# Layer 1 of a four-layer kernel: how the planes a and b go to HBM and come back

## The chip, the cores and the metric

One core of one Trainium2 chip runs the whole program in one launch. The metric is the device time of an execution in microseconds (us). The core has a matrix engine (TensorE, PE; its weight loads are listed as PEld), three engines for elementwise work (VectorE, DVE; ScalarE, ACT; GpSimd, POOL), SyncE (SP), which here only issues DMAs, and 16 DMA engines, which move data between HBM and the on-chip memory (SBUF, 128 partitions). Matmul results land in PSUM.

## The reference, cut to what matters

The input x has 256 x 256 tokens of 128 channels. Four layers follow each other, each `x = x + layer(groupnorm(x))`: triangle attention (layer 0), a triangle multiplication over 16 channels (layer 1), a second one over 128 channels (layer 2), and a chain of convolutions (layer 3). The change lies in layer 1:

```python
a = jax.nn.sigmoid((x @ Wa1 + ba1) * (x @ Wa2 + ba2))   # 16 channels
b = jax.nn.sigmoid((x @ Wb1 + bb1) * (x @ Wb2 + bb2))
g = jax.nn.sigmoid(x @ Wg + bg)
z = jnp.einsum('bikc,bkjc->bijc', a, b)                 # per channel: a 256 x 256 times 256 x 256 product
return g * (_ln(z, ln2_g, ln2_b) @ Wz + bz)
```

All data are float32. The products with the weights need x with channels on the partitions; the product in `z` needs, for each of the 16 channels, a whole 256 x 256 plane with tokens on the partitions. Between the two, a and b go through HBM.

## The kernel before, in words

The 65,536 tokens are cut into 32 pieces of 2048 (`SC`), a piece into four chunks of 512 (`CK`). The layers run one behind the other. In layer 1 the engines' orders are written out by hand (`manual_schedule`): instructions run on each engine in the order of the code. The whole stage is three loops.

*Making a and b (pool `p3`, lines 828 to 877).* The result of layer 0, channels by tokens, lies in HBM as `x1T`. Thirteen slots in SBUF hold pieces of it; eight are loaded before the loop (line 778, `load1`), five at its head, and the loop over pieces, with index i, loads piece i+13 into the slot that piece i has left. For a piece, eight groups of matmuls (line 859) with 32 output rows each (16 of a, 16 of b) write the four chunks q of both factors to partitions 32q to 32q+31 of two PSUM tiles `p1`, `p2`. ACT copies the first with its bias (line 868), DVE multiplies by the second (line 869), and one step later ACT takes the sigmoid into `p3_ab` (line 842, `close3`), a tile of 128 x 512 of which there are 12 buffers. Row 32q + c holds channel c (0 to 15 of a, 16 to 31 of b) of chunk q. `store3` (line 848) sends it to HBM three steps after the piece's matmuls: four DMAs of 32 rows, those for q = 0 and 1 on POOL's queue, those for q = 2 and 3 on SP's. Each row is 2 KB. So on SP a step issues the load of piece i+13, then two stores for piece i-3. After the last load, which is followed by the stores of piece 15, only stores are left.

The tensor `abD` in HBM has 32 rows, one per channel, each 65,536 tokens long plus 1024 of padding; within a row the order is chunk number q, then piece s, then the 512 tokens t of the chunk.

*The product (pool `z`, lines 881 to 936).* Channels are taken in pairs g. `load_z(g)` fetches two planes of a and two of b into one of three buffers: both planes of a by one DMA of 512 KB (line 893; a row's 128 stretches of 512 tokens go to the 128 partitions in the order in which they lie, so partition 32q + s holds chunk q of piece s), and each plane of b by one of 256 KB in the order of the tokens (line 895; partition 4s + q). Three pairs are fetched ahead; a later one, k // 2 + 3, after the second plane k of a pair. For each plane, four transposes on PE turn a (`tri_turn`, line 1807), ACT copies the result (line 1809), and eight matmuls multiply (`tri_multiply`, line 1818). The transposes of plane k+1 stand ahead of the product of plane k. DVE, ACT and POOL collect sums for the layer norm (lines 914 to 926); the sixteen planes are normalized and sent to HBM (line 936).

*The last loop (pool `p4`)* multiplies by `Wz`, applies the gate and adds to x.

Two rules set the order of the DMAs. The first load of a waits for all stores to `abD`. And the build gives each queue's DMAs eight semaphores in turn, so a DMA on SP is issued only when the one eight places before it on SP has landed; POOL's DMAs have eight of their own. A sigmoid waits until the store of the piece twelve before it has landed, because it writes the same buffer.

The parts of the code that the change touches:

Of the kernel before, what the change touches and what calls it, by code (L numbers as in the profile page):

```python
# [9 lines left out]
F32 = mybir.dt.float32  # L10
# [6 lines left out]
P = 128  # L17
N = 256
D = 128
T = N * N  # L20
SC = 2048
NSC = T // SC
CK = 512
NH = 4
HC = 32
PAD = 1024
# [6 lines left out]
def kernel(ctx: ExitStack, tc: tile.TileContext, a: dict, out: bass.AP):  # L33
    nc = tc.nc
# [4 lines left out]
    dram = ctx.enter_context(tc.tile_pool(name="dram", bufs=1, space=DRAM))  # L39

    def rows(name, n):

        return dram.tile([n, T + PAD], F32, name=name)[:, 0:T]
# [3 lines left out]
    rsD = dram.tile([1, T], F32, name="rsD")  # L47
    mbD = dram.tile([N, N], F32, name="mbD")
    x1T = rows("x1T", D)
    abD = rows("abD", 32)  # L50
    znD = rows("znD", 16)
    x2T = rows("x2T", D)

# [184 lines left out]
    with tc.tile_pool(name="x0", bufs=1) as xres, tc.tile_pool(name="p0", bufs=3) as sb:  # L238
        held = {s: xres.tile([P, SC], F32, name=f"x0_{s}") for s in range(RES, NSC)}
        with tc.tile_pool(name="p0ps", bufs=3, space=PSUM) as ps, tc.tile_pool(  # L240
            name="f0ps", bufs=2, space=PSUM
# [167 lines left out]
        with tc.tile_pool(name="p1", bufs=2) as wk_sb, tc.tile_pool(  # L409
            name="p1ps", bufs=4, space=PSUM  # L410
# [70 lines left out]
    with tc.tile_pool(name="p2e", bufs=6) as eb, tc.tile_pool(name="p2c", bufs=1) as cs:  # L481
        triT = cs.tile([P, NH, 2, N], F32, name="triT")
        with tc.tile_pool(name="p2", bufs=2) as sb, tc.tile_pool(
            name="p2S", bufs=2, space=PSUM
        ) as psS, tc.tile_pool(name="p2z", bufs=1, space=PSUM) as psZ, tc.tile_pool(
            name="p2M", bufs=3, space=PSUM
        ) as psM, ExitStack() as by_hand:
            groups = {}
            rows = {}
# [213 lines left out]
            for j in range(2 * NG + 5):  # L703
                g, half = divmod(j, 2)
# [71 lines left out]
    def load1(s, slot):  # L776
        xs[s] = slots[slot].tile([P, SC], F32, name="x1", tag="x1")
        nc.sync.dma_start(xs[s], x1T[:, s * SC : (s + 1) * SC])
# [54 lines left out]
    with x1_scope:  # L833
        with tc.tile_pool(name="p3", bufs=3) as sb, tc.tile_pool(
            name="p3ps", bufs=3, space=PSUM
        ) as ps, tc.manual_schedule():
            halves, done = [], []

            def close3():
                s, s1 = halves.pop(0)  # L840
                ab = sb.tile([P, CK], F32, name="p3_ab", bufs=12)
                nc.scalar.activation(ab, s1, AF.Sigmoid)
                done.append((s, ab))

            def store3():
                s, ab = done.pop(0)
                for q in range(4):
                    (nc.gpsimd if q < 2 else nc.sync).dma_start(
                        abD.rearrange("c (q s t) -> q s c t", q=4, t=CK)[q, s], ab[32 * q : 32 * q + 32, :]
                    )  # L850

            for i in range(FIRST, SLOTS):
                load1(order1[i], i)
            for i, s in enumerate(order1):
                p1 = ps.tile([P, CK], F32, name="p3_1")
                p2 = ps.tile([P, CK], F32, name="p3_2")
                for pp, w in ((p1, v1), (p2, v2)):
                    for c in range(4):
                        nc.tensor.matmul(
                            pp[32 * c : 32 * c + 32, :], lhsT=w, rhs=xs[s][:, c * CK : (c + 1) * CK],  # L860
                            start=True, stop=True,
                        )
                if i + SLOTS < NSC:
                    load1(order1[i + SLOTS], i % SLOTS)
                if len(done) > 1:
                    store3()
                s1 = sb.tile([P, CK], F32, name="p3_s1")
                nc.scalar.activation(s1, p1, AF.Identity, bias=vb1)
                nc.vector.scalar_tensor_tensor(s1, p2, vb2, s1, ALU.add, ALU.mult)
                halves.append((s, s1))  # L870
                if i:
                    close3()
            close3()
            while done:
                store3()
# [4 lines left out]
        with tc.tile_pool(name="z", bufs=2) as sb, tc.tile_pool(  # L880
            name="zps", bufs=3, space=PSUM
        ) as ps, tc.manual_schedule():
            Z = sb.tile([P, 16, 2 * N], F32, name="z_Z", bufs=1)
            s1 = sb.tile([P, 2 * N], F32, name="z_s1", bufs=1)
            s2 = sb.tile([P, 2 * N], F32, name="z_s2", bufs=1)
            base = sb.tile([P, 2 * N], F32, name="z_base", bufs=1)
            AB = {}

            def load_z(g):
                if g < 8:  # L890
                    ab = gate_pool.tile([P, 4, 2 * N], F32, name="z_ab", tag="g")
                    AB[g] = A, B = ab[:, 0:2, :], ab[:, 2:4, :]
                    nc.sync.dma_start(A, abD[2 * g : 2 * g + 2, :].rearrange("c (p t) -> p c t", p=P))
                    for c in range(2):
                        nc.sync.dma_start(
                            B[:, c, :], abD[16 + 2 * g + c, :].rearrange("(q s t) -> s q t", q=4, t=CK)
                        )

            def turn_z(k):
                if k < 16:  # L900
                    return tri_turn(nc, ps, sb, AB[k // 2][0], k % 2, ident, nc.scalar.copy)

            for g in range(3):
                load_z(g)
            nc.vector.memset(Z[:, 0, :], 0.0)
            at = turn_z(0)
            for k in range(16):
                nxt = turn_z(k + 1)
                pz = tri_multiply(nc, ps, at, AB[k // 2][1], k % 2).rearrange("p t n -> p (t n)")
                at = nxt  # L910
                if k % 2 == 1:
                    load_z(k // 2 + 3)
                if k == 0:
                    nc.vector.tensor_copy(base, pz)
                    continue
                z = Z[:, k, :]
                nc.vector.tensor_tensor(z, pz, base, ALU.subtract)
                sq = s2 if k == 1 else sb.tile([P, 2 * N], F32, name="z_sq")
                nc.scalar.activation(sq, z, AF.Square)
                if k == 1:  # L920
                    nc.vector.tensor_copy(s1, z)
                    continue
                nc.vector.tensor_tensor(s1, s1, z, ALU.add)
                if k < 15:
                    nc.gpsimd.tensor_tensor(s2, s2, sq, ALU.add)

            nc.vector.scalar_tensor_tensor(s1, s1, -1.0 / 16, s1, ALU.mult, ALU.mult)
            nc.vector.tensor_tensor(s2, s2, s1, ALU.add)
            nc.vector.tensor_tensor(s2, s2, sq, ALU.add)
            nc.vector.tensor_scalar(s2, s2, 0.0, None, ALU.max)  # L930
            nc.scalar.activation(s2, s2, AF.Sqrt, bias=epst, scale=1.0 / 16)
            nc.vector.reciprocal(s1, s2)
            for q in range(4):
                zq = Z[:, 4 * q : 4 * q + 4, :]
                nc.vector.tensor_tensor(zq, zq, s1.unsqueeze(1).to_broadcast([P, 4, 2 * N]), ALU.mult)
                nc.sync.dma_start(znD[4 * q : 4 * q + 4, :].rearrange("c (p t) -> p c t", p=P), zq)
# [4 lines left out]
        with tc.tile_pool(name="p4", bufs=3) as sb, tc.tile_pool(  # L941
            name="p4psg", bufs=2, space=PSUM
# [46 lines left out]
            for i, s in enumerate(order):  # L989
# [5 lines left out]
                for c in range(4):  # L995
                    q = slice(32 * c, 32 * c + 32)
# [83 lines left out]
    with tc.tile_pool(name="x5", bufs=7) as x5_pool, tc.tile_pool(name="p5", bufs=2) as sb, tc.tile_pool(name="p5psX", bufs=1, space=PSUM) as psX, tc.tile_pool(  # L1080
        name="p5psM", bufs=3, space=PSUM
# [89 lines left out]
        for s in range(NSC):  # L1171
            b, j = divmod(s, KB)
            load5(s + 7)
            ab = [sb.tile([P, SC], F32, name=n) for n in ("p5_a", "p5_b")]
# [55 lines left out]
    with tc.tile_pool(name="p6", bufs=3) as sb, tc.tile_pool(name="p6ps", bufs=3, space=PSUM) as ps:  # L1230
        nc.vector.memset(k1, 0.0)
        nc.gpsimd.memset(k2, 0.0)
        with tc.manual_schedule():
# [16 lines left out]
            for c in range(D):  # L1250
                q = c // 4
# [21 lines left out]
    with tc.tile_pool(name="p7", bufs=2) as sb, tc.tile_pool(name="p7psX", bufs=2, space=PSUM) as psX, tc.tile_pool(  # L1273
        name="p7psM", bufs=2, space=PSUM
# [142 lines left out]
    with tc.tile_pool(name="p9", bufs=2) as sb, tc.tile_pool(name="p9psM", bufs=2, space=PSUM) as psM, tc.tile_pool(  # L1417
        name="p9psX", bufs=2, space=PSUM
# [382 lines left out]
def tri_turn(nc, ps, sb, A, c, ident, evacuate):  # L1801

    Ac = A[:, c, :].rearrange("p (t k u) -> p t u k", t=2, u=2)
    pa = ps.tile([P, 2, N], F32, name="tp_a")
    for u in range(2):
        for t in range(2):
            nc.tensor.transpose(pa[:, u, t * P : (t + 1) * P], Ac[:, t, u, :], ident)  # L1807
    at = sb.tile([P, 2, N], F32, name="tp_at")
    evacuate(at, pa)  # L1809
    return at  # L1810


def tri_multiply(nc, ps, at, B, c):
    Bc = B[:, c, :].rearrange("p (u n) -> p u n", u=2)
    pz = ps.tile([P, 2, N], F32, name="tp_z")
    for t in range(2):
        for u in range(2):
            nc.tensor.matmul(  # L1818
                pz[:, t, :], lhsT=at[:, u, t * P : (t + 1) * P], rhs=Bc[:, u, :], start=(u == 0), stop=(u == 1)
            )  # L1820
    return pz
# [38 lines left out]
```

## Time and profile before

Four runs took 3407.88 to 3417.56 us, with a median of 3410.55.

| | |
|---|---|
| profiled execution | 3411.61 us |
| its span (first to last instruction) | 3409.9 us |
| mean granted PE clock | 0.957 |
| busy share of the span: PE, DVE, ACT, POOL | 92%, 66%, 59%, 47% |
| loop that makes a and b | from about 1505 to 1589 us |
| loop of the product | from about 1589 to 1628 us |
| stores to `abD` | 64 from POOL, 64 from SP, 64 KB each |
| issue of one such store on POOL | 496 ns |
| loads from `abD` | 8 of 512 KB (a), 16 of 256 KB (b) |

Times are from the start of the span. In the rows of a timeline, the first two numbers are start and length in us, then come engine, line, operation, output <- input, how many equal ones were merged (x), and in brackets how long the engine had been idle and what ended that. "SPq" is the queue of SP: the length there is that of issuing DMAs, not that of the transfers. In the window table each row is a stretch of time, with the busy time and the number of instructions of each engine, the granted clock of PE (1.00 is full), the mean busy share of the 16 DMA engines, and the rate at which they moved data. The busy share of a whole execution is a mean over stages with different limits; the two loops here take about 120 of the 3410 us.

### The profile page before, as it was taken

Reading aid. Unit: us, or ns where it says so; the run is one execution under the profiler, and the core shown is the slowest. Engines: PE = TensorE matmul, PEld = TensorE weight load, DVE = VectorE, ACT = ScalarE, POOL = GpSimd, SP = SyncE. Lnnn points to the kernel's source line nnn. Section 1 sums busy time; section 2 is a strip of 40 time slices with the busy share of each in tenths; the row PEclk is TensorE's granted clock in tenths of the full one; section 3 lists DMA queues with packets and bytes.
Section 4 is the critical chain, followed back from the end, with each engine's and each line's share of the span. In section 5 each row is a group of like instructions: output and inputs, shape, how many; then the busy total and the mean of one; then the engine's idle time right before and its main releaser. Section 6 shows DMA issues by size and latency. Waiting matters only on the chain. (4 is left out here: it accounts for less than half of the span.)

```text
span 3409.9 us, 52669 instructions
## 1 busy us (share of the span) xinstructions
PE 3121.2 (92%) x20266; PEld 1649.6 (48%) x20266; DVE 2263.1 (66%) x2608; ACT 2014.1 (59%) x2204; POOL 1618.6 (47%) x930
## 2 busy tenths in 40 slices
PE   5669999999999999966886999999999999769998
PEld 5425555555555555523332444444999433224444
DVE  5627888888888888843554545444555677747776
ACT  3657777777777777733575444443444466636565
POOL 4146777777777777733463000000555344514334
PEclk8889999999999999978996999999999999979999
DMA  9972333333333333278596668756999899756664
GB/s 393 365 292 72 122 110 119 107 119 109 117 114 112 119 107 119 95 302 317 213 380 269 260 224 298 284 210 252 349 353 350 304 336 334 277 165 198 202 197 131
DMA packets 298235, 750.06 MB, mean 220 GB/s; under 512 B 74954, under 2 KB 145580, under 8 KB 248828
## 3 DMA queue, kind: packets, MB, share of 16 engines
q1 hardware_dynamic: 289371, 734.19, 60.3%
q0 software_dynamic: 8096, 10.86, 0.9%
q8 instruction: 162, 2.65, 0.3%
q10 hardware_dynamic: 512, 1.59, 0.1%
q14 instruction: 94, 0.76, 0.1%
HBM read 458.88 MB, written 287.66 MB: 219 GB/s over the span
## 5 line engine op out<-in xcount | busy, mean ns | idle before, releaser
L564 DVE TENSOR_TENSOR p_e<-p_S,triT 128x1024 f32<-128x1024 f32 x512 | 608.9, 1211 | 144.9 <-PE p_S L554 144.9
L574 POOL TENSOR_TENSOR p_es<-p_e 128x1024 f32<-128x1024 f32 x256 | 603.5, 2369 | 126.2 <-issue 66.6
L572 ACT ACTIVATE p_e<-p_e,mbT 128x1024 f32<-128x1024 f32 x512 | 552.0, 1138 | 61.3 <-DVE p_e L564 61.2
L1152 PE MATMUL p_pm<-p_zn,wf 128*128 128x512 f32 x1040 | 450.2, 595 | 1.4 <-DVE p_zn L1169 1.4
L539 PE MATMUL p_mm<-p_xn,w 128*128 128x512 f32 x768 | 407.3, 614 | 0.3 <-DVE p_v L534 0.3
L1152 PEld LDWEIGHTS p_pm<-p_zn,wf 128*128 128x128 f32 x1040 | 197.6, 191 | 254.9 <-issue 248.0
L554 PE MATMUL p_S<-p_q,p_k 32*128 32x256 f32 x4096 | 295.9, 401 | 3.5 <-DVE p_e L564 3.2
L1554 POOL TENSOR_TENSOR p_q<-p_q,p_pb 128x2024 f32<-128x2024 f32 x32 | 144.1, 4504 | 257.1 <-DVE p_pb L1548 257.1
L554 PEld LDWEIGHTS p_S<-p_q,p_k 32*128 32x128 f32 x4096 | 186.2, 184 | 159.6 <-PE p_mm L530 91.7
L1818 PE MATMUL tp_z<-p_B,tp_at 128*128 128x256 f32 x1024 | 251.1, 388 | 1.0 <-DVE tp_at L1809 1.0
L513 POOL TENSOR_TENSOR p_xn<-p_xn,p_rs 128x1024 f32<-128x1024 f32 x63 | 151.0, 2397 | 208.8 <-ACT p_xn L508 126.9
L587 PE MATMUL p_o<-p_e,p_v 128*32 128x256 f32 x4096 | 249.1, 384 | 0.0
L1218 POOL DMA_DIRECT2D rs__17959<-rs2D x4 | 2.0, 502 | 511.9 <-DVE p_zn L1145 511.9
L1261 POOL TENSOR_TENSOR k<-k,p_sq 128x512 f32<-128x512 f32 x128 | 162.9, 1273 | 158.0 <-ACT p_sq L1259 158.0
L1371 POOL TENSOR_TENSOR p_x<-p_x,p_g 128x2048 f32<-128x2048 f32 x30 | 136.3, 4543 | 161.2 <-DVE p_g L1358 112.5
L1818 PEld LDWEIGHTS tp_z<-p_B,tp_at 128*128 128x128 f32 x1024 | 185.6, 191 | 23.6 <-DVE tp_at L1809 1.8
L539 PEld LDWEIGHTS p_mm<-p_xn,w 128*128 128x128 f32 x768 | 126.5, 191 | 105.6 <-issue 89.9
L587 PEld LDWEIGHTS p_o<-p_e,p_v 128*32 128x32 f32 x4096 | 120.4, 110 | 110.2 <-ACT p_g L545 41.5
L1260 DVE TENSOR_TENSOR k<-tp_z,k 128x512 f32<-128x512 f32 x128 | 88.6, 692 | 128.0 <-ACT p_sq L1259 128.0
L1257 ACT COPY p_K<-tp_z 128x512 f32<-128x512 f32 x128 | 74.9, 585 | 158.8 <-PE tp_z L1818 158.8
L545 ACT ACTIVATE p_g<-p_mm,bgh 128x512 f32<-128x512 f32 x128 | 87.9, 687 | 131.8 <-PE p_mm L539 131.7
L1185 DVE SCALAR_TENSOR_TENSOR p_b<-p_pm,b2w,p_b 128x1024 f32<-128x1024 f32 x64 | 82.1, 1283 | 125.5 <-PE p_pm L1152 111.1
(372 smaller groups left out, 5961.6 us busy)
## 6 DMA issues: line engine op xcount, KB each, us to landing
p_x<-x2T SPq DMA_DIRECT2D x60, 1024.0 KB
x<-x1T SPq DMA_DIRECT2D x51, 1024.0 KB
p_x<-in_x_dram SPq DMA_DIRECT2D x32, 1024.0 KB
p_x<-xT SPq DMA_DIRECT2D x64, 512.0 KB
x2T<-x SPq DMA_DIRECT2D x32, 1024.0 KB
aD<-p_a SPq DMA_DIRECT2D x32, 1024.0 KB
bD<-p_b SPq DMA_DIRECT2D x32, 1024.0 KB
p_A<-aD SPq DMA_DIRECT2D x32, 1024.0 KB
```

Of the source, the lines that this page charges most:

```text
L513: nc.gpsimd.tensor_tensor(xn, xn, groups[g]["rs"], ALU.mult)
L539: nc.tensor.matmul(pm, lhsT=w, rhs=t["xn"][:, cs_], start=True, stop=True)
L554: nc.tensor.matmul(Ss[h // 2][:, h % 2, u, :], lhsT=t["k"][hp, r * N + u * P : r * N + (u + 1) * P], rhs=t["q"][hp, r * N : (r + 1) * N], ...
L564: nc.vector.tensor_tensor(e[:, :, 2 * p : 2 * p + 2, :].rearrange("p u h n -> p h u n"), Ss[p], triT[:, 2 * p : 2 * p + 2, :, :], ALU.add,)
L572: nc.scalar.activation(e[:, u, :, :], e[:, u, :, :], AF.Exp, bias=mbT[:, u, i : i + 1])
L574: nc.gpsimd.tensor_tensor(es, e[:, 0, :, :], e[:, 1, :, :], ALU.add)
L587: nc.tensor.matmul(t["o"][hp, r % 2, :], lhsT=t["v"][:, r * 2 + u, hp], rhs=e[:, u, h, :], start=(u == 0), stop=(u == 1),)
L1152: nc.tensor.matmul(pm[:, c, :], lhsT=wf2[:, i, :], rhs=zns[s][:, k * CK : (k + 1) * CK], start=True, stop=True)
L1261: nc.gpsimd.tensor_tensor(k2, k2, sq, ALU.add)
L1371: nc.gpsimd.tensor_tensor(xs7[s], xs7[s], gts[s], ALU.add)
L1554: nc.gpsimd.tensor_tensor(q[:, :, 1 : N - 2], q[:, :, 1 : N - 2], pb[:, :, 0 : N - 3], ALU.add)
L1818: nc.tensor.matmul(pz[:, t, :], lhsT=at[:, u, t * P : (t + 1) * P], rhs=Bc[:, u, :], start=(u == 0), stop=(u == 1))
```

## The change

`abD` becomes a tensor of 128 rows, in the layout of the tile `p3_ab` itself: row 32q + c holds chunk q of channel c for all 32 pieces, 16,384 tokens, and again 1024 of padding. The distance between two rows in HBM falls from 266,240 to 69,632 bytes. A piece is stored by one DMA of 128 rows of 2 KB, on SP. POOL issues none of them any more.

A plane's four chunks now lie in four rows 32 apart. The two planes of a in a pair are therefore fetched by four DMAs of 128 KB, one per chunk number q, each into 32 partitions; what lands where in SBUF is as before. A plane of b is still fetched by one DMA, with other strides in HBM. On SP, the loop that makes a and b issues one store per step instead of two, and each `load_z` issues six DMAs instead of three. The instructions of PE, ACT and DVE, and their order, stay the same; some of them wait for other semaphores.

```diff
-    abD = rows("abD", 32)
+    abD = dram.tile([P, T // 4 + PAD], F32, name="abD")[:, 0 : T // 4]
...
             def store3():
                 s, ab = done.pop(0)
-                for q in range(4):
-                    (nc.gpsimd if q < 2 else nc.sync).dma_start(
-                        abD.rearrange("c (q s t) -> q s c t", q=4, t=CK)[q, s], ab[32 * q : 32 * q + 32, :]
-                    )
+                nc.sync.dma_start(abD[:, s * CK : (s + 1) * CK], ab)
...
                     AB[g] = A, B = ab[:, 0:2, :], ab[:, 2:4, :]
-                    nc.sync.dma_start(A, abD[2 * g : 2 * g + 2, :].rearrange("c (p t) -> p c t", p=P))
+                    for q in range(4):
+                        r = slice(32 * q + 2 * g, 32 * q + 2 * g + 2)
+                        nc.sync.dma_start(
+                            A[32 * q : 32 * q + 32, :, :], abD[r, :].rearrange("c (s t) -> s c t", t=CK)
+                        )
                     for c in range(2):
                         nc.sync.dma_start(
-                            B[:, c, :], abD[16 + 2 * g + c, :].rearrange("(q s t) -> s q t", q=4, t=CK)
+                            B[:, c, :], abD.rearrange("(q c) (s t) -> c s q t", q=4, t=CK)[16 + 2 * g + c]
                         )
```

## The prediction

> **What bounds the kernel now.** I read the window table around layer 1's two stages first, then the timelines of ScalarE (ACT), SP's queue and TensorE (PE) where they meet, and last the waits. The window table (columns: window and its length; busy time and count of PE, PEld, DVE, ACT, POOL; granted clock; DMA share; GB/s):
>
> ```profile
> 1500.00:1574.00 74.00, 59.84 (x518) 21.80 (x518) 22.71 (x38) 35.34 (x58) 26.02 (x53) 0.94 1.01 413
> 1574.00:1589.00 15.00, 2.06 (x20) 0.50 (x16) 3.00 (x4) 4.54 (x8) 5.59 (x12) 0.72 0.66 200
> 1589.00:1600.00 11.00, 7.07 (x27) 6.01 (x28) 1.18 (x2) 1.76 (x3) 0.00 (x0) 0.60 0.85 286
> 1600.00:1628.00 28.00, 28.00 (x155) 25.45 (x155) 17.48 (x26) 13.64 (x25) 14.03 (x11) 1.00 0.60 188
> ...
> 1578.00:1580.00 2.00, 0.00 (x0) 0.00 (x0) 1.50 (x2) 1.70 (x5) 1.78 (x5) 1.00 0.73 217
> 1584.00:1586.00 2.00, 0.00 (x0) 0.00 (x0) 0.00 (x0) 0.00 (x0) 0.00 (x0) 0.50 0.54 148
> 1594.00:1596.00 2.00, 2.00 (x8) 1.48 (x7) 0.00 (x0) 1.17 (x2) 0.00 (x0) 0.50 1.03 386
> ```
>
> Until 1574 the stage that makes a and b is bound by DMA (share 1.01). From 1574 to 1589 no engine has much to do and DMA is only two thirds busy: this hole is what the change can fill. From 1600 PE is busy without a gap, so the z loop is PE's. The timelines of ACT, SP and PE say what the hole is:
>
> ```profile
> 1575.74 0.63 ACT L842 ACTIVATE p_ab<-p_s 128x512 f32<-128x512 f32 x1 [1.75 <-DMA abD<-p_ab]
> ...
> 1579.96 0.63 ACT L842 ACTIVATE p_ab<-p_s 128x512 f32<-128x512 f32 x1 [0.30 <-DVE p_s L869]
> 1566.61 21.04 SPq L848 DMA_DIRECT2D abD<-p_ab  x34
> 1583.98 3.67 SPq L848 DMA_DIRECT2D abD<-p_ab  x8
> 1589.08 0.38 SPq L893 DMA_DIRECT2D z_ab<-abD  x1
> 1589.51 1.42 SPq L895 DMA_DIRECT2D z_ab<-abD  x2
> 1592.93 1.95 PE L1807 MATMUL tp_a<-ident,z_ab 128*128 128x128 f32 x8 [15.87 <-DMA z_ab<-abD]
> 1598.06 0.63 PE L1807 MATMUL tp_a<-ident,z_ab 128*128 128x128 f32 x4
> 1600.45 0.37 SPq L893 DMA_DIRECT2D z_ab<-abD  x1
> 1606.85 0.63 PE L1807 MATMUL tp_a<-ident,z_ab 128*128 128x128 f32 x4
> ```
>
> The last sigmoid ends at 1580.59, but SP still issues 64 KB stores until 1587.65, one per 0.46 us (3.67/8): 64 KB per 0.46 us is 143 GB/s, the 148 of that window. SP's issue, not DMA and not ACT, sets this end. The last lands at 1589.08, the first load of a goes out, and PE starts 3.85 us later. The waits (us in total, times, longest) name the other half of the mechanism:
>
> ```profile
> ACT p_ab L842 <- DMA abD<-p_ab: 23.0, 12, 2.2
> ```
>
> p_ab has 12 buffers, so piece j's sigmoid waits for the store of piece j-12. The wait that ends at 1575.74 is piece 27's (four more follow it), for the store of piece 15, the first behind the last load in SP's order.
>
> **The sum.** The profiled execution took 3411.61 us, a span of 3409.9 and 1.7 around it; the median of the runs shown is 3410.55, 1.06 lower. I reckon on the profile's time and take 1.06 off at the end.
>
> *While loads run (1500 to 1574).* Per piece one load of 1 MB and 256 KB of stores, before and after; DMA is full, so the rate, about 3.1 us a piece, stays. SP drops from three issues to two a piece, at 0.30 to 0.38 us, hidden since SP waits there for loads. SP issues a DMA only when the one eight before it has landed; eight outstanding are then 4 loads and 4 stores instead of 2.7 and 5.3 halves, deeper, so DMA stays fed. POOL loses 64 issues of 0.50 us (32 us); nothing waits for POOL in this stage but these stores: zero. One thing moves: POOL's halves no longer run ahead. At 1575 POOL has sent its halves up to about piece 25, ten pieces ahead of SP: 10 x 128 KB = 1.31 MB, at 413 GB/s 3.2 us. Now piece 15's store has only loads and pieces 0 to 15 before it and lands at 1575.74 - 3.2 = 1572.5; the last sigmoid follows five ACT rounds of 1.1 us later, about 1578.
>
> *The tail.* Sixteen stores of 256 KB remain (pieces 16 to 31), all on SP, at most 16 x 0.46 = 7.4 us of issues, so DMA sets the pace. No row shows a 128-row store of 2 KB rows alone. Bounds: the fastest DMA seen here, 432 GB/s in the slice 1566 to 1568, gives 0.61 us each, 9.7 in all; the busiest slice of the present tail, 278 GB/s at 1580 to 1582, gives 0.94 and 15.1. The nearest row is the loads of a and b at 1592 to 1598 (128 rows, 2 KB runs, SP alone): about 375 GB/s, 0.70 us each, 11.2. I take that: the last lands at 1572.5 + 11.2 = 1583.7 instead of 1589.08, **-5.4 us** (ends -6.9 and -1.5). Cross-check by bytes: the DMA share over 1574 to 1589 is 0.66 x 15 = 9.9 us of work, so a full DMA ends near 1584.
>
> *Start of the z loop.* Plane pair 0 of a now comes by four DMAs of 128 KB. The last is issued 3 x 0.46 = 1.4 us after the first. Today's 3.85 us hold 1.4 us of data (512 KB at 375) and 2.45 around it; now 1.4 + 2.45 + 0.35 (128 KB) = 4.2, **+0.35**. The low end is 0 (SP issues faster, four already stream); the high end, if a 32-partition DMA moved only the tail's 148 GB/s, is 4 x 0.89 + 2.45 = 6.0, +2.15. I take **+0.6**, near the low end, because the 148 was SP's pace. [...]
>
> B waits behind them on SP: its first plane goes out at 1.8 instead of 0.43 us, lands at 1.8 + 2.45 + 0.7 = 5.0, and is used at 5.75 (1594.83): hidden. Pair 1's a: last issue at about 4.6, landing 7.4, used at 1598.06, 9.0 after the start: hidden, 1.6 to spare.
>
> *Within the loop.* Each pair makes six issues (2.7 us) instead of three. Pair 3's go out at 1600.45 and plane 6 is transposed at 1606.85: 6.4 us of cover against 4.2 needed (6.0 at the slow rate): zero.
>
> *Clock.* The granted clock falls to 0.50 in PE's pause and is back at 1.00 by 1598 to 1600. The pause stays about 14 us, so the slow restart stays: zero. All behind the z loop shifts as it is.
>
> Sum: -5.4 + 0.6 = -4.8, so 3406.8 on the profile and 3405.8 against the median: **3406 us**, 0.13% faster. A measurement of this kernel tells about 0.2% (7 us) from no change, so this counts as the same.
>
> **Rivals.**
> 1. *A full gain, over 0.2%.* The tail runs at 432 GB/s (-6.9), the quarters cost nothing, and one queue instead of two lets the loaded part run at 432 instead of 413 GB/s: 4% of the roughly 50 us in which DMA alone paces it, -2.0. Total -8.9, 3401.6. For it: the hole is real and POOL's queue is gone. Against: three ends at once, and 1.01 already looks full.
> 2. *The lead gives nothing back.* If piece 15's store lands at 1575.7 as now (one queue behind more outstanding loads), the last lands at 1575.7 + 11.2 = 1586.9: -2.2 + 0.6 = -1.6, 3409. For it: every store now stands behind loads. Against: the bytes that POOL sent early must go somewhere.
> 3. *Slower: whole stores to rows 68 KB apart run slowly.* The 128 rows of a store have a new row distance, and no trace shows it. If a 256 KB store kept the 148 GB/s of the present tail (1.77 us), sixteen take 28.3 us, the last lands at 1600.8, +11.7 + 0.6 = +12.3: 3422.9. It decides from 1.0 us a store (262 GB/s; 1572.5 + 16 x 1.0 + 0.6 is today's 1589.1). For it: no window of stores alone in this stage exceeds 278 GB/s. Against: those windows are paced by SP's issues.
> 4. *The z loop becomes load-bound.* At 0.89 us a quarter, a pair costs 3.6 + 1.4 = 5.0 us of DMA against 4.4 of PE: 5 x 0.6 = +3.0 over pairs 3 to 7 and +2.15 at the start, against -5.4: 3410.3, no change.
>
> **How the numbers follow.** My forecast (-1.9 to -6.5, and its neighbour within noise) 0.48; rival 1 0.27; rivals 2 and 4 together 0.16; rival 3 0.09. Runs of one kernel spread by some 9 us, their median by about 2, so a true -4.8 is read beyond -6.8 now and then; that is in the 0.27. Faster 0.27, same 0.64 (forecast and rivals 2 and 4), slower 0.09. The range runs from rival 1 (3401) to just above rival 4 with that noise (3412); outside lie rival 3 and the far half of rival 1. The likeliest case's own range is 3404 to 3409.
>
> **What would show it.** Right: SP's last store lands near 1584 (1582 to 1588), DMA share over 0.9 from 1574 until then, ACT's last wait on the store of piece 15 ends near 1572.5, no POOL stores, PE's first transpose some 4.2 to 4.8 us after SP's first load of a, and PE without gaps after it. Wrong: stores landing one per 1.0 us or more (rival 3), gaps in PE ahead of every second plane's transposes, ended by loads of a (rival 4), or a later landing of piece 15's store (rival 2).

## The result, and the profile after

The changed kernel took 3403.58 us, the median of 42 runs (3393.61 to 3414.89), against 3410.98 for 63 runs of the kernel before (3402.86 to 3422.86). The ratio is 0.9979, with a 95% interval of 0.9974 to 0.9985: 7.2 us less (5.1 to 8.9). The profiled execution after took 3404.6 us (span 3402.9), 7.0 less than the one before. The forecast was -4.8. The time lies in the stated range (3401 to 3412) and on its fast side: just below the 3404 to 3409 that I had called the likeliest case's own range, and with 0.21% just beyond the 0.2% that I had called no change.

The window table of the kernel after, around the two stages (columns as before: busy time and count of PE, PEld, DVE, ACT, POOL; granted clock; DMA share; GB/s):

```profile
1500.00:1574.00 74.00, 61.30 (x534) 17.34 (x534) 23.46 (x39) 36.59 (x61) 0.00 (x0) 0.94 1.01 414
1574.00:1585.00 11.00, 0.11 (x4) 0.00 (x0) 2.74 (x4) 3.33 (x6) 0.00 (x0) 0.63 0.75 284
1585.00:1596.00 11.00, 8.42 (x38) 7.05 (x39) 1.81 (x3) 2.38 (x5) 0.00 (x0) 0.75 0.95 269
1596.00:1624.00 28.00, 28.00 (x153) 25.28 (x152) 17.41 (x26) 13.76 (x27) 15.31 (x12) 1.00 0.64 189
...
1578.00:1580.00 2.00, 0.00 (x0) 0.00 (x0) 0.00 (x0) 0.00 (x0) 0.00 (x0) 0.50 1.06 408
1590.00:1592.00 2.00, 1.86 (x7) 1.22 (x6) 0.10 (x1) 0.00 (x0) 0.00 (x0) 0.85 1.02 271
1592.00:1594.00 2.00, 1.86 (x10) 1.73 (x11) 0.59 (x1) 0.59 (x1) 0.00 (x0) 1.00 1.06 277
```

While loads run nothing changed: share 1.01, 414 GB/s (413 before), though POOL, busy 26 us there before, now does nothing. The hole behind it is filled: stores alone keep DMA at share 1.06 and 408 GB/s, where the same stage had 217 and 148 GB/s. New is the start of the z loop: DMA is as full as before (1.02 to 1.06) but moves 271 to 277 GB/s instead of 386.

The timelines of ACT, SP's queue and PE give the ends:

```profile
1572.79 0.63 ACT L842 ACTIVATE p_ab<-p_s 128x512 f32<-128x512 f32 x1 [1.89 <-DMA abD<-p_ab]
1577.00 0.63 ACT L842 ACTIVATE p_ab<-p_s 128x512 f32<-128x512 f32 x1 [0.30 <-DVE p_s L866]
...
1560.38 18.78 SPq L847 DMA_DIRECT2D abD<-p_ab  x17
1583.18 1.74 SPq L892 DMA_DIRECT2D z_ab<-abD  x4
1584.97 1.25 SPq L896 DMA_DIRECT2D z_ab<-abD  x2
1586.26 2.00 SPq L892 DMA_DIRECT2D z_ab<-abD  x4
...
1587.30 1.95 PE L1808 MATMUL tp_a<-ident,z_ab 128*128 128x128 f32 x8 [13.19 <-DMA z_ab<-abD]
1592.14 0.75 PE L1808 MATMUL tp_a<-ident,z_ab 128*128 128x128 f32 x4 [0.27 <-DMA z_ab<-abD]
1594.45 0.63 PE L1808 MATMUL tp_a<-ident,z_ab 128*128 128x128 f32 x4
```

ACT's last wait for a store ends at 1572.79 (1575.74 before), SP's last store is issued by 1579.16, all stores have landed at 1583.18 when the first load of a goes out (1589.08 before), and PE starts 4.12 us later (3.85 before). PE's second pair waits 0.27 us for a at 1592.14, which it did not before; its later pairs do not.

So the changed stage itself is worth -5.7 us in this pair of profiles, but the kernel gained 7.0. Followed through the pair (start of an event after minus before, from the timelines):

| event | after minus before, us |
|---|---|
| first matmul of the stage that makes a and b | -0.2 |
| SP's first load of a | -5.9 |
| PE's first transpose of a | -5.6 |
| last product of the z loop | -5.8 |
| first product of layer 1's last loop | -3.9 |
| start of layer 2 | -2.5 |
| start of layer 3 | -3.9 |
| last product of layer 3 | -7.0 |

Two things are in it that the forecast did not have: about 2 us are given back right behind the z loop, and 4.5 us come in layers 2 and 3, where no instruction differs. (Another 1.4 us go in layer 1's last loop of this pair; in three profiles of each kernel, below, they do not.) The experiments were chosen for these two and for the terms of the sum.

### The profile page after: what moved, and what is told of

It is laid out like the page before. It is cut to its first block, busy times and chain, and to the rows that moved or that the text cites. A ratio compares the mean times of both kernels' runs of the same rounds, so it can differ in the third digit from the quotient of the medians.

```text
span 3402.9 us, 52543 instructions
## 1 busy us (share of the span) xinstructions
PE 3122.8 (92%) x20266; PEld 1647.7 (48%) x20266; DVE 2263.1 (67%) x2608; ACT 2014.6 (59%) x2204; POOL 1588.4 (47%) x866
## 4 chain that ended last, share of the span: by engine, by line
PE 40%; DMA 6%; DVE 2%; ACT 1%; POOL 1%; issue 1%; SPq 1%; ACTq 0%; DVEq 0%; POOLq 0%
PE p_pm L1153 13%; PE tp_z L1819 7%; PE p_pm L1306 6%; PE p_pm L1541 5%; DMA x2T<-x 2%; PE tp_a L1808 2%; PE p_st L1110 1%; PE p_pg L971 1%; PE p_pt L1578 1%; PE p_rz L1067 1%; POOL x L1019 1%; DMA p_er<-eD 1%; DMA p_x<-x3T 1%; PE p_rk L1067 1%; PE p_eb L1067 1%
## 5 line engine op out<-in xcount | busy, mean ns | idle before, releaser
L539 PE MATMUL p_mm<-p_xn,w 128*128 128x512 f32 x768 | 407.3, 614 | 0.3 <-DVE p_v L534 0.3
L1186 DVE SCALAR_TENSOR_TENSOR p_b<-p_pm,b2w,p_b 128x1024 f32<-128x1024 f32 x64 | 82.2, 1284 | 125.5 <-PE p_pm L1153 111.1
```

Source lines behind the costliest of these rows:

```text
L539: nc.tensor.matmul(pm, lhsT=w, rhs=t["xn"][:, cs_], start=True, stop=True)
```

## The experiments

Each kernel was also compared with the kernel before on the same chip. I quote the intervals of the trace that the disputes turn on. "Stage" is from the first matmul of the a/b stage to SP's first load of a; "start" from there to PE's first transpose; "z stores" from the issue of the four 1 MB stores of `znD` (behind the z loop) to the issue of the next load, which waits until they have landed; "layer 3" from its first to its last product. All in us, one profiled execution each; the lengths are differences of times that are read to a tenth.

| kernel | stage | start | z stores | layer 3 | ratio to before [95%] |
|---|---|---|---|---|---|
| before | 83.6 | 3.85 | 11.88 | 416.9 | |
| before, second profile | 85.0 | 3.67 | 11.88 | 413.8 | |
| before with later addresses | 85.1 | 3.82 | 11.88 | 420.8 | 1.0008 [0.9997, 1.0020] |
| before, 24 more transposes | 85.9 | 3.82 | 11.88 | 410.8 | 0.9994 [0.9984, 1.0005] |
| after | 77.9 | 4.12 | 13.63 | 413.8 | 0.9979 [0.9974, 0.9985] |
| after, second profile | 77.9 | 4.29 | 13.54 | 410.2 | 0.9982 [0.9971, 0.9992] |
| after with the old addresses | 78.1 | 4.31 | 13.65 | 410.2 | 0.9987 [0.9978, 0.9996] |
| new layout, old stores | 84.6 | 4.61 | 13.49 | 410.3 | 1.0006 [0.9994, 1.0018] |
| four stores, all on SP | 113.3 | 4.16 | 13.46 | 411.0 | 1.0084 [1.0068, 1.0099] |
| after, 24 more transposes | 80.3 | 4.40 | 11.91 | 413.4 | 0.9977 [0.9968, 0.9986] |
| after, 40 transposes in the pause | 77.8 | 4.23 | 11.90 | 412.5 | 0.9998 [0.9988, 1.0008] |
| one store, old layout | 140.4 | 3.90 | 11.87 | 410.7 | (one time, 3459.72) |
| two stores of 64 rows | 86.1 | 4.20 | 13.65 | 407.3 | 0.9998 [0.9989, 1.0008] |
| two stores of 1 KB rows | 82.2 | 4.17 | 13.46 | 408.7 | 0.9989 [0.9978, 1.0000] |

### Do the new addresses of everything behind `abD` matter?

The new tensor is 393 KB larger, so all later tensors move in HBM. One kernel gives after a smaller padding, so that they lie where they lay before; the other moves them in before.

```diff
-    abD = dram.tile([P, T // 4 + PAD], F32, name="abD")[:, 0 : T // 4]
+    abD = dram.tile([P, T // 4 + 256], F32, name="abD")[:, 0 : T // 4]
```

> The changed kernel with 256 instead of 1024 tokens of padding per row of abD. The tensor then has the size that it had before, so every HBM tensor behind it lies at its old address; rows are 66,560 bytes apart. Theory (all of the gain is made at the stores' tail, -5.8 us at the first transposes of the z loop, and what differs behind it is scatter of the DMA-bound stages): the same as the changed kernel, -5 to -8 us against before, ratio about 0.998. Rival (the tensors behind abD have moved by 393,216 bytes in HBM, and later stages are faster by some 3 us for that): only -3 to -5 us, ratio about 0.999. Either way SP's first load of a comes at about 1583 us.

```diff
-    abD = rows("abD", 32)
+    abD = dram.tile([1, 32 * (T + PAD) + 98304], F32, name="abD")[:, 0 : 32 * (T + PAD)]
+    abD = abD.rearrange("o (c t) -> (o c) t", c=32)[:, 0:T]
```

> The kernel before with abD made 393,216 bytes larger, unused, so that every HBM tensor behind it lies where the changed kernel has it; nothing else differs. Theory (tail of the stores): 0, within 2 us of before, and SP's first load of a at about 1589 us. Rival (addresses): -1.5 to -3 us, made in layer 3 and the last loop of layer 1.

Measured: after with the old addresses has a median of 3401.24 against 3406.45, keeps z stores at 13.65 and has a layer 3 of 410.2, as short as in the second profile of after. Before with the new addresses has 3410.99 against 3406.45 (1.0008, not told from 1), z stores at 11.88 and the longest layer 3 of all (420.8). The longer z stores stay with the code and not with the addresses, and the short layer 3 does not come with the new addresses either. By its time alone the first kernel does not decide: its ratio of 0.9987, -4.4 us, lies in the rival's -3 to -5, and the interval (-7.5 to -1.4) holds most of the other range too. The second speaks against the rival, whose -1.5 to -3 lie outside its interval (-1.0 to +6.8).

### Stores or loads: which part carries the gain?

New layout and new loads, with the old store routine (four DMAs of 32 rows, two of them on POOL):

```diff
-                nc.sync.dma_start(abD[:, s * CK : (s + 1) * CK], ab)
+                for q in range(4):
+                    r = slice(32 * q, 32 * q + 32)
+                    (nc.gpsimd if q < 2 else nc.sync).dma_start(abD[r, s * CK : (s + 1) * CK], ab[r, :])
```

> The changed kernel with its layout and its four loads of a per pair, but stores as before: four of 32 rows, two on POOL, two on SP. It prices the loads alone. Theory: SP's first load of a at 1589 us as before, PE's first transpose 0.3 to 0.6 us later after it than the 3.85 us of before, no gaps in the z loop: +0.3 to +0.6 us against before, not to be told from 0. [...]

Measured: 3408.45 against 3406.45, 1.0006 [0.9994, 1.0018]. The stage is as long as in before (84.6), the start 0.8 us longer than before's 3.85, the z stores 1.6 us longer. So the stores carry the whole gain of the stage; the new loads by themselves cost 2.4 us by these two rows, where I had expected 0.3 to 0.6, and the ratio cannot tell either from nothing.

### Is it the number of DMAs, the queue or the number of rows?

The new kernel with four stores per piece, all on SP:

```diff
-                nc.sync.dma_start(abD[:, s * CK : (s + 1) * CK], ab)
+                for q in range(4):
+                    r = slice(32 * q, 32 * q + 32)
+                    nc.sync.dma_start(abD[r, s * CK : (s + 1) * CK], ab[r, :])
```

> The changed kernel with its layout, but each piece stored by four DMAs of 32 rows, all four on SP. If SP's issue (0.46 us each, one at a time) sets the tail, 64 issues behind the store of piece 15 take 29.4 us instead of 11: SP's first load of a at about 1602 us, +19 against the changed kernel, +12 to +14 against before. If bytes alone set it, nothing differs from the changed kernel (-7). Five DMAs a piece, eight outstanding, may also hold back the loads earlier; a DMA share under 0.95 between 1520 and 1570 us would show that, and would add to the loss.

Measured: 3436.11 against 3406.45, 1.0084 [1.0068, 1.0099]: +28.6 to before by the ratio, twice what I expected. The window table of this kernel, and its timeline of SP:

```profile
1520.00:1570.00 50.00, 38.55 (x317) 9.78 (x313) 13.67 (x19) 21.22 (x35) 0.00 (x0) 0.89 0.95 326
1570.00:1616.00 46.00, 13.08 (x80) 2.65 (x72) 5.26 (x7) 9.59 (x16) 0.00 (x0) 0.65 0.62 189
1595.00:1605.00 10.00, 0.00 (x0) 0.00 (x0) 0.00 (x0) 0.36 (x1) 0.00 (x0) 0.50 0.51 139
...
1589.66 26.58 SPq L849 DMA_DIRECT2D abD<-p_ab  x56
1617.68 1.73 SPq L894 DMA_DIRECT2D z_ab<-abD  x4
```

In the tail SP issues one store per 0.47 us (26.58/56), and 64 KB per 0.47 us is the 139 GB/s of the third row: SP's pace again, as in before, only for all stores. What I had named but not put into the number is the first row: while loads still run, the rate falls from 414 to 326 GB/s at a share of 0.95. My estimate from the order of issue: five issues a piece through eight outstanding places leave only 1.6 loads of 1 MB under way. (In the trace of after, SP's DMAs use eight semaphores in turn, and from 1510 to 1625 us each of 90 went out only when the one eight before it had landed.)

Two ways to cut a piece in two, both with 32 stores left for the tail: two halves of the rows, or two halves of the columns.

```diff
-                nc.sync.dma_start(abD[:, s * CK : (s + 1) * CK], ab)
+                for q in range(2):
+                    r = slice(64 * q, 64 * q + 64)
+                    nc.sync.dma_start(abD[r, s * CK : (s + 1) * CK], ab[r, :])
```

> The changed kernel with each piece stored by two DMAs of 64 rows (partitions 0 to 63, then 64 to 127), both on SP. If only the number of issues counts, 32 issues of 0.46 us behind the last load's store take 14.7 us instead of 11: +3 to +4 us against the changed kernel (first load of a some 81 to 82 us after the first matmul of the stage instead of 77.9). [...]

```diff
-                nc.sync.dma_start(abD[:, s * CK : (s + 1) * CK], ab)
+                for h in range(2):
+                    nc.sync.dma_start(
+                        abD[:, s * CK + 256 * h : s * CK + 256 * h + 256], ab[:, 256 * h : 256 * h + 256]
+                    )
```

> The changed kernel with each piece stored by two DMAs of 128 rows, each with half of the tokens (1 KB a row), both on SP: as many issues and bytes per DMA as with two of 64 rows, but over all partitions. Issue theory: +3 to +4 us against the changed kernel, 32 issues of 0.46 us. [...] If rows of 1 KB are themselves slower, the DMA share stays near 1 in the tail at a rate under 380 GB/s, and the loss is larger.

The window table of the kernel with halves of 64 rows (loads running, then stores alone):

```profile
1520.00:1560.00 40.00, 33.40 (x301) 9.15 (x293) 12.65 (x17) 20.09 (x34) 0.00 (x0) 1.00 1.02 421
1572.00:1582.00 10.00, 0.00 (x0) 0.00 (x0) 0.00 (x0) 0.00 (x0) 0.00 (x0) 0.50 0.89 205
```

And of the kernel with halves of the columns (stores alone):

```profile
1574.00:1584.00 10.00, 0.00 (x0) 0.00 (x0) 0.50 (x1) 0.87 (x2) 0.00 (x0) 0.50 0.74 259
```

Same bytes, same number of issues, same queue. With all 128 rows and 1 KB runs the tail is paced by SP (share 0.74, 259 GB/s; 128 KB per 0.5 us) and the stage is 4.3 us longer than after's. With 64 rows of 2 KB it moves 205 GB/s, half of after's 408, at a share of 0.89: the engines are nearly full and yet slow, and the stage is 8.2 us longer. So both the number of issues and the number of rows count. The halves of the columns cost what the issues were expected to; the halves of the rows cost twice that, and why 64 rows go at half of the rate was not shown. While loads run alongside, neither costs anything (421 GB/s with 64 rows, 413 with halves of the columns).

### Would one store in the old layout have done?

Against the kernel after, with the loads of before:

```diff
-    abD = dram.tile([P, T // 4 + PAD], F32, name="abD")[:, 0 : T // 4]
+    abD = rows("abD", 32)
...
-                nc.sync.dma_start(abD[:, s * CK : (s + 1) * CK], ab)
+                nc.sync.dma_start(abD.rearrange("c (q s t) -> s q c t", q=4, t=CK)[s], ab)
```

> The kernel before with its layout and its loads, but each piece stored by one DMA of 128 rows on SP (in HBM four groups of 32 rows). It asks whether the new layout was needed. If only the number of issues matters, it behaves as the changed kernel: -5 to -8 us. [...]

Measured, in a single execution: 3459.72, 52.6 above the median of before on that chip (3407.14). The window table and SP's timeline of this kernel:

```profile
1520.00:1570.00 50.00, 33.38 (x266) 12.82 (x262) 11.28 (x15) 16.78 (x28) 0.00 (x0) 0.90 0.72 273
1620.00:1632.00 12.00, 0.00 (x0) 0.00 (x0) 0.00 (x0) 0.00 (x0) 0.00 (x0) 0.50 0.26 102
...
1581.85 49.26 SPq L847 DMA_DIRECT2D abD<-p_ab  x17
1642.00 0.39 SPq L890 DMA_DIRECT2D z_ab<-abD  x1
```

DMA is a quarter busy, 0.26, at 102 GB/s, at which one store of 256 KB takes 2.6 us. In the new layout such a store, alone as here, ran at 408 GB/s and a share of 1.06. Both kernels send as many stores, of the same 128 rows of SBUF and on the same queue; in HBM the rows lie in four groups of 32 here and as 128 rows there. Why the four groups go at a quarter of the rate was not shown, but the new layout is a part of the gain and not a side matter. (With the old loads, the z stores are at 11.87.)

### What is given back behind the z loop?

The DMA view of the kernel after from 1636 to 1650 us, in 40 slices of 0.35 us (rate, then the queues with packets, MB and share of the 16 engines):

```profile
GB/s 0 0 0 0 129 404 427 392 421 410 404 416 380 421 410 363 398 410 386 416 415 398 421 398 398 433 386 415 427 380 433 404 398 392 41 23 23 29 23 6
...
q1 hardware_dynamic: 2112, 4.19, 77.3%
q8 instruction: 1, 0.02, 0.5%
issues: line engine op xcount, KB each, median us to landing
znD<-z_Z SPq DMA_DIRECT2D x4, 1024.0 KB
```

The four stores move at some 400 GB/s and then go on for five slices at 23 to 41 GB/s, about the rate of a single engine (a sixteenth of 400 is 25). In the same window one 16 KB packet of an instruction queue ran; its 0.5% of 16 engines and 14 us is 1.1 us of one engine. My estimate from these rates is that one of the 16 engines ended late with its part of the stores, and the next load waited for it. No view names the engine; that it is the one that moved the packet, and why it would fall 1.75 us behind for a packet of 1.1 us, was not shown. In before's window, from 1642 to 1654 us in slices of 0.30 us, there is no such packet and no such end:

```profile
GB/s 0 0 0 0 130 389 416 416 416 389 416 416 416 376 410 430 416 382 410 430 416 382 410 430 403 396 410 430 403 396 410 416 396 410 416 416 396 410 369 7
...
q1 hardware_dynamic: 2112, 4.19, 89.9%
```

SP's timelines differ by that much: before,

```profile
1642.49 6.96 SPq L936 DMA_DIRECT2D znD<-z_Z  x4
1654.37 2.60 SPq L954 DMA_DIRECT2D p_z<-znD  x4
```

and after:

```profile
1636.68 6.96 SPq L937 DMA_DIRECT2D znD<-z_Z  x4
1650.31 2.60 SPq L955 DMA_DIRECT2D p_z<-znD  x4
```

11.88 against 13.63 us. To try it, 24 transposes of the identity into a spare PSUM tile, whose results nobody uses, were added while PE waits for DMA in the a/b stage. They push PE's later instructions back in its instruction stream:

```diff
+            spare = ps.tile([P, P], F32, name="p3_spare", bufs=1)
...
+                if i >= 20:
+                    for _ in range(2):
+                        nc.tensor.transpose(spare, ident, ident)
```

> The changed kernel with 24 extra transposes of the identity into a spare PSUM tile, two each in the last 12 pieces of the loop that makes a and b, where PE waits for loads anyway. They only lengthen PE's instruction stream ahead of the z loop. Theory: the 16 KB instruction fetch, which the changed kernel has in the middle of the stores of the normalized planes, comes some 48 PE instructions earlier, ahead of them, and the stretch from the first of those stores to the next loads shrinks from 13.6 to 11.9 us: -1.75 us against the changed kernel, about -9 against before if the rest stays. Rival (the longer stretch has another cause, such as the layout): it stays at 13.5 and nothing changes.

The DMA view of this kernel from 1635 to 1648 us (slices of 0.325 us), and its SP timeline:

```profile
GB/s 0 0 139 410 403 410 416 403 410 416 403 416 416 410 410 403 416 403 403 403 410 410 403 403 416 410 403 403 416 416 422 410 410 403 82 0 0 0 0 0
...
q1 hardware_dynamic: 2112, 4.19, 83.0%
```

```profile
1634.91 6.97 SPq L941 DMA_DIRECT2D znD<-z_Z  x4
1646.82 2.60 SPq L959 DMA_DIRECT2D p_z<-znD  x4
```

No packet, no tail at 23 GB/s, 11.91 us. In the table all seven kernels with a packet in the window have 13.46 to 13.65 us and all seven without it 11.87 to 11.91; the packet goes with 1.6 to 1.8 us more than before's 11.88. And it follows the loads: every kernel with four DMAs for a pair of a has it, unless transposes were added; every kernel with one DMA has not. Why the four DMAs move the place was not shown. The time of this kernel, 3399.41 against 3407.14 for before and 3400.06 for after on the same chip, is not told apart from after's. Nor is its layer 1 shorter, for its stage took 80.3 us, 2.4 more than after's. Here a 16 KB packet ran at 1569.0, among the stores of a and b, and their last 2 us (1578.6 to 1580.6) moved only 14 to 55 GB/s. But two kernels with such a packet among these stores have no longer stage (after with the old addresses, at 1570.4, and after with 40 transposes, at 1575.3), so what lengthened this one stays open.

The same 24 transposes in before should have brought the packet into its window:

```diff
+            spare = ps.tile([P, P], F32, name="p3_spare", bufs=1)
...
+                if i >= 20:
+                    for _ in range(2):
+                        nc.tensor.transpose(spare, ident, ident)
```

> The kernel before with the 24 extra transposes, two in each of the last 12 pieces, that moved the instruction fetch out of the stores of the normalized planes in the changed kernel. Theory (the position of PE's instruction stream decides where the fetch falls): here they move it from the first products after those stores into them; the stretch from the first store to the next loads grows from 11.9 to 13.6 us: +1.75 us, the rest of the kernel as before. Rival (the stretch is a matter of the layout or of the loads of a): it stays 11.9. If the position of the instruction stream is also what makes layer 3 some 6 us shorter in the other variants, layer 3 takes 410 to 414 here and the sum is -4 us.

A miss: the z stores stay at 11.88. The packet came 43.5 us after the first load of a, ahead of the stores, so this kernel says nothing about the cost of the fetch. Its ratio is 0.9994 [0.9984, 1.0005], in which no cost of the transposes shows. Layer 3 took 410.8 us, but the -4 us that I had tied to that are neither shown nor ruled out (-5.5 to +1.7).

### Can the start of the z loop be had at full clock?

PE stands still for some 13 us ahead of the z loop and its clock falls to 0.50. Forty transposes of the identity, added work again, were put into the pause, and some loads of a on ACT's queue:

```diff
-                        nc.sync.dma_start(
+                        (nc.scalar if q > 1 and g < 3 else nc.sync).dma_start(
...
+            spare = ps.tile([P, P], F32, name="z_spare", bufs=1)
+            for _ in range(40):
+                nc.tensor.transpose(spare, ident, ident)
```

> The changed kernel with two additions: 40 transposes of the identity into a spare PSUM tile ahead of the z loop, while PE waits for the last stores (11 us of work in a pause of 13), and for the first three pairs the two DMAs of a for partitions 64 to 127 issued on ACT's queue instead of SP's. Theory: the granted clock stays at 1.00 at the start of the z loop; planes of a for pair 0 land some 0.5 us and for pair 1 about 1 us earlier; the fetch moves ahead of the stores of the normalized planes. In sum -2 to -4 us against the changed kernel, -9 to -11 against before. Rival: the start of the z loop is bound by the loads' bytes and the clock changes nothing: only the fetch's -1.75 remains.

The timeline of PE and the window table of this kernel:

```profile
1577.52 6.25 PE L909 MATMUL z_spare<-ident 128*128 128x128 f32 x40 [2.92 <-DVE p_s L866]
1587.89 1.93 PE L1811 MATMUL tp_a<-ident,z_ab 128*128 128x128 f32 x8 [4.12 <-DMA z_ab<-abD]
...
1582.00:1584.00 2.00, 1.77 (x17) 1.53 (x14) 0.13 (x1) 0.00 (x0) 0.00 (x0) 1.00 0.12 44
1584.00:1586.00 2.00, 0.00 (x0) 0.00 (x0) 0.36 (x1) 0.00 (x0) 0.00 (x0) 1.00 0.63 179
1588.00:1594.00 6.00, 5.35 (x16) 4.17 (x17) 0.00 (x0) 1.17 (x2) 0.00 (x0) 0.50 1.06 284
```

It failed. The forty took 6.25 us (I had reckoned 11) and did bring the clock back to 1.00, but they ended at 1583.77, a pause of 4.12 us followed, and at 1588, 4.3 us after the last of them and just after PE had restarted, the clock fell to 0.50 and stayed there until 1594. The restart is not what brings the fall: in the thirteen other profiles it comes while PE stands still, 2.0 to 4.3 us after its last matmul (in after 2.8 us: the clock of 1576 to 1578 is 0.74, and PE's last matmul ended at 1574.11; in before 3.6 us: the clock of 1580 to 1581 is 0.82, and it ended at 1577.06). A longer burst might have held the clock; none was tried. The fourth plane's transposes came 8.7 us after the start, against 7.15 in after and 8.0 and 8.1 in its second profile and its variant with the old addresses. Nor did a second queue raise the rate: 284 GB/s at a share of 1.06. So SP's issue is not what makes the quarters slow; what does was not shown. The z stores are free of the packet here (11.90), and still the kernel is no faster than before: 0.9998 [0.9988, 1.0008].

### How much does one profile of before say?

The unchanged kernels once more, after beside the kernels above and before with one time:

> The changed kernel unaltered, beside the next three on one chip, and a second profile of it. Theory: SP's first load of a 5.5 to 6 us earlier than before, counted from the first matmul of the stage; the four stores of the normalized planes again last 13.6 us from the first issue to the next loads' first issue (11.9 before), with a 16 KB instruction fetch among them; layer 3 scatters, its length from the first product to the end anywhere between 410 and 421 us. If the extra gain in layer 3 belongs to the change, it is 410 to 414 us again.

> The kernel before unaltered: a second profile of it. From the first product of layer 3 to the end, the first profile took 416.9 us and the variant with moved addresses 420.8, while eight profiles of other variants took 410.2 to 413.8. If that is scatter, this one may lie anywhere from 410 to 421; if the kernel before is slower there by itself, 416 to 421 again. The stores of the normalized planes last 11.9 us to the next loads again, with no 16 KB instruction fetch among them.

After: 3400.06 against 3407.14, stage 77.9, z stores 13.54. Before: stage 85.0, z stores 11.88. With the address variants that makes three profiles of each. Stage: 84.6 and 77.95 in the mean, **-6.6**. Start: 3.78 and 4.24, **+0.46**. From PE's first transpose to the z loop's last product: 37.1 and 38.3, **+1.2** (after 37.3, 39.4, 38.3; before 37.5, 36.8, 37.0). These follow the clock more than the loads: in the first 8 us from PE's first transpose it is 0.79, 0.61 and 0.60 in after's three, and 0.70, 0.79 and 0.76 in before's, and in two of after's three PE waits for no load after its first. (The clock does not explain 39.4 against 38.3.) From there to the first product of the last loop of layer 1, which holds the z stores: 30.3 and 32.9, **+2.6**. The last loop to the start of layer 2: **-0.2**. Together -2.5 when layer 2 begins. Then layer 2: 1146.3 and 1145.0, **-1.3**. Layer 3: 417.2 and 411.4, **-5.8**, with single values from 410.2 to 420.8.

Layer 3 is the largest single difference and is not settled. It does not follow the addresses (above), nor the packet's place: kernels with it have 407 to 414, kernels without it 411 to 421. Nor is it tied to the kernel's median: before with 24 transposes and the new layout with old stores have 410.8 and 410.3 and are no faster than before. The second profile of before has 413.8, the first 416.9. The stage that makes a and b begins anywhere from 1497.3 to 1507.8 in these profiles, ahead of any changed instruction, so a single profile carries several us of scatter that has nothing to do with the change.

Much of the spread goes with the execution that the profile caught. Before with later addresses was caught in the slowest of its eleven runs (3417.68, median 3410.99), and the kernel with 64-row stores, whose layer 3 is the shortest (407.3), in the fastest of its ten (3401.57, median 3407.44). The three profiled executions of each kind differ by 12.1 us in the mean, the medians of many runs by 7.4. So the means of three overstate what lies behind layer 1; the first pair, whose times lie 0.6 and 1.0 us above their medians, is the better guide there.

## Why the prediction was right, and where it was not

*The loaded part costs nothing.* Right: 413 to 414 GB/s, share 1.01, and POOL's absence cost nothing.

*POOL's lead comes back.* Right, to 0.3 us: the store of piece 15 landed at 1572.79, 1572.5 forecast. Rival 2 (1575.7) is out.

*The tail.* Right in mechanism: DMA, not SP's issue, sets it. First load of a at 1583.18, 1583.7 forecast. Stores alone ran at 408 GB/s; I had taken the loads' 375 as the nearest row, and from 1572.79 on the sixteen took 0.65 us each instead of 0.70. Rival 3, slow stores by the row distance, is out by the same row. In three profiles a kind, the term is -6.6 where I had -5.4 (ends -6.9 and -1.5): inside, near the fast end, which supposed 432 GB/s.

*Start of the z loop.* +0.27 in the pair, +0.46 in the mean, against +0.6. The slower loads that the high end supposed were seen: 271 to 277 GB/s at full share (1.02 to 1.06), in a place where 386 was moved before, but well above the 148 of that end. Why they are slower was not shown.

*Pair 1's a hidden with 1.6 us to spare.* Wrong: it landed some 8.9 us after SP's first load of a and not 7.4, and PE waited 0.27 us for it, though not in the two other profiles. The later pairs are hidden, PE is busy without a gap from 1596 to 1624, and rival 4 is out.

*The clock, at zero.* Right in the pair (0.79 against 0.70 in the first 8 us of the loop), but a matter of luck: in the two other profiles of after it came back later, and the loop took 38 to 39 us instead of 37.

*"All behind the z loop shifts as it is."* This is the step that failed. Behind it the kernel lost about 2 us at the z stores, by a 16 KB instruction fetch that the new loads moved into their window (shown: it went when the stream was moved). Then layers 2 and 3 were 4.5 us shorter in the pair (7.1 in the mean of three, which overstates it), for a cause that stays open.

So the size was off twice in opposite ways. Layer 1 as a whole accounts for -2.5 of the -7.0 in the pair, about half of the -4.8 that I had summed up there; that the time came within 2.4 us of the forecast is in part luck. (With layer 1 alone it would have been 3408, also in the range.) The comparison of many runs (-7.2, interval -8.9 to -5.1; -6.1 and -4.4 in two further comparisons, the second with the old addresses) says that the whole is larger than layer 1's share. Part of the difference may be scatter of the profiles; how much, these runs do not tell. That the median was nearer to rival 1 (-8.9) than to the forecast is not that rival's doing: neither the quarters for free nor a faster loaded part was seen.

## What to carry to other kernels

Where a stage ends in stores alone, look at DMA share and rate in that tail: a share well under 1 with one queue issuing back to back (0.54 here) meant that fewer and larger DMAs helped, and a share near 1 with a low rate (0.89 at 205 GB/s) or near a quarter (0.26 at 102 GB/s) went with stores of 64 rows, or of four groups of 32 rows in HBM, where 128 rows on both sides ran at 408 GB/s. So try 128 rows on both sides of the store, even if the tensor in HBM has to be laid out anew for it and the loads get smaller where they are hidden. A forecast that shifts everything behind the change unaltered is good to a few us only: look for bulk transfers that something waits for, expect the place of instruction fetches to move (here one of 16 KB came among such stores, which then took 13.63 us instead of 11.88), and compare each profiled execution with the median of its kernel before trusting a length read from it.

## What the runs showed of the hardware

- A 16 KB instruction fetch (a packet of 0.95 to 1.1 us) in the middle of four 1 MB stores went with 13.5 to 13.65 us from their first issue to the next load's, instead of 11.9, in seven profiles against seven; in after they end at 23 to 41 GB/s, where a sixteenth of 400 is 25.
- Stores of 128 rows of 2 KB, issued back to back, ran at 408 GB/s; the same bytes in 64-row DMAs at 205, in 32-row DMAs at 139 (there by the issue, 0.47 us each), and in 128-row DMAs whose HBM side is four groups of 32 rows at 102.
- Five issues a piece on one queue instead of two, with as many bytes, cut the loaded part from 414 to 326 GB/s; that the eight outstanding DMAs of a queue are the reason is argued.
- Forty transposes raised the clock to 1.00 and did not hold it over the 4.12 us pause behind them: it fell to 0.50 at 1588, 4.3 us after the last of them, and stayed there for some 7 us. In the thirteen other profiles it fell 2.0 to 4.3 us after PE's last matmul, with PE still idle.
